# Causal attention with a routed feed-forward on one core: the softmax sums are accumulated on GpSimd and multiplied by ones once per step

## The chip, the core and the metric

One core of a Trainium2 chip runs the whole program. TensorE (PE) multiplies matrices into PSUM, VectorE (DVE) and ScalarE (ACT) do elementwise work, reductions and exponentials, GpSimd (POOL) does elementwise work on SBUF, and SyncE (SP) issues the transfers. Each engine works through its own queue of instructions; semaphores tie them together. The metric is the device time of one execution in microseconds (us), as the median of a few runs. One further execution is recorded by the profiler, and its instructions are what the views below show.

## The reference

The input x has two sequences of 2048 tokens with 512 features, all in float32. The layer is

- x = x + attention(layernorm(x)), with 16 heads of width 32, rotary positions on queries and keys, a causal mask and a softmax over the keys;
- x = x + ffn(layernorm(x)), where ffn is a 512x512 linear layer with a bias plus a routed low-rank part: eight experts of rank 16, of which a softmax router picks two per token.

The part that matters here is the softmax: for each query and head, the sum over all keys of exp(score - shift) times the value row, divided by the sum over all keys of exp(score - shift). The second sum, the denominator, is what the change moves.

## The kernel before, in words

The tokens are cut into eight **blocks** n = 0..7 of 512 (four per sequence; j = n mod 4 is the place of the block in its sequence), the heads into four **groups** g of four heads. A **step** (n, g) is the attention of one block's queries for one group, 32 steps in all. Step (n, g) looks at 4(j+1) **key tiles** of 128 keys: 4, 8, 12 or 16. The last four lie on the diagonal.

Work on one step has two passes. In the first (`row_maxima`, line 346) PE computes scores with queries on the partitions (`sm`, line 367) and DVE takes the row maxima (lines 375 and 380), which are turned (line 397) into a shift. In the second (`attend`, line 432) PE computes the scores again with keys on the partitions (`sc`, line 463), adds the shift by a small matmul (line 471), and ACT takes the exponential (line 485) into a buffer `pt` that holds one key tile for four heads, 128 x 4 x 512 in float32. On diagonal tiles POOL then sets the masked corner to zero, two heads at a time (line 494). PE multiplies the tile with the values into the PSUM bank `av` (line 519). The four heads of a group sit in different rows or columns of the PE array and run side by side; a float32 matmul shows as two records. The fourth diagonal tile shares a buffer with the second, so that a step of 16 tiles has 15 exponential stages, called quads.

The denominator: when both tiles of a pair (0,1), (2,3), ... have been multiplied, POOL adds the odd tile onto the even one in two instructions of two heads each (line 534), and three phases later PE multiplies the pair's sum by a 128x32 tile of ones into the PSUM bank `den` (`summed`, line 545), accumulating over the pairs. After the last pair ACT copies the sums out (line 554), a chain of small transfers with a reciprocal on DVE in between (lines 567 to 579) spreads 1/sum over the partitions, and POOL scales the context (line 581).

The order of PE, ACT and DVE is written out by the program: the second pass of a step runs beside the first pass of the next one, half a quad of each at a time (`side_by_side`, line 591), and after each half, called a phase, a loop (lines 733 to 763) may place other work. That is the value and denominator matmuls that have come due (`later`, `between`, `ahead`) and stages of other blocks, paced by a credit in us: projections of the next block (`kps`, `qps`, lines 182 to 201, whose rotary part ends with two POOL instructions; `vps`), and the output projection and feed-forward of the former block (`ops`, `xnps`, `mid`, `yps`, lines 227 to 340, with small POOL chains for the layernorm and the bias). These stages are called fillers below. The order of POOL and SP follows from it.

Buffers: `pt` has four (`PTS`). PSUM has a ring of six banks for scores and fillers (`bank`), beside `av` and `den`. `before()` (line 500) forces due work out of the list before the buffers that it holds are taken again. `wo` and `base_w`, the 1 MB weights of the output projection and of the linear layer, are loaded once at the start.

## Time and profile before

| | |
|---|---|
| median of 3 runs | 1982.68 us (1980.56 to 1984.05) |
| profiled execution, whole | 1982.82 us |
| its span | 1981.0 us |
| PE busy | 1918.0 us (97%) |
| PE weight loads | 731.2 us (37%) |
| POOL busy | 1008.7 us (51%) |
| DVE busy | 1018.2 us (51%) |
| ACT busy | 768.0 us (39%) |
| pair additions on POOL (line 534) | 320 instructions, 609.9 us busy |
| denominator matmuls (line 545) | 1280 records, 163.3 us busy |

Busy is the time in which at least one instruction of a kind ran. PE instructions overlap, so their mean times exceed what each adds: for 1280 records of the denominator the mean is 569 ns, but eight records that belong to one pair keep PE busy for about 1.1 us.

A step's end is easy to find in the timeline: the ACT copy of `av` at line 538. The stretches between these copies are called the steps' lengths below. For blocks 2 and 3, in us: (2,0) 61.3, (2,1) 77.8, (2,2) 65.6, (2,3) 75.5, (3,0) 82.8, (3,1) 92.7, (3,2) 79.7, (3,3) 75.7. For blocks 6 and 7: 61.3, 76.8, 65.6, 75.5, 81.7, 84.3, 72.8 and 54.4. They differ within a block because the fillers are not spread evenly. The last step has neither fillers nor a first pass beside it. What follows the last copy takes 52.2 us.

### The profile page before, as it was taken

How to read it: one execution, taken by the hardware profiler on the slowest of the kernel's cores; microseconds unless marked ns; L12 is line 12 of the kernel's file. 1: busy time of each engine (PE TensorE's matmuls, PEld its weight loads, DVE VectorE, ACT ScalarE, POOL GpSimd, SP SyncE). 2: the span in 40 equal slices, each digit the busy share in tenths (PEclk: the TensorE clock that was granted, in tenths of full speed). 3: DMA queues.
4: the chain of work that ended last, by engine and by line, in shares of the span. 5: the costliest groups of instructions: out<-in, count | busy, mean ns of one | idle time of the engine just before them, and what ended most of it. 6: DMA issues, size and time to landing. Idle time of an engine off the chain costs nothing.

```text
span 1981.0 us, 31399 instructions
## 1 busy us (share of the span) xinstructions
PE 1918.0 (97%) x12256; PEld 731.2 (37%) x12256; DVE 1018.2 (51%) x2760; ACT 768.0 (39%) x1601; POOL 1008.7 (51%) x906
## 2 busy tenths in 40 slices
PE   7999999999999999999999999999999999999997
PEld 3433433333333333333343434333433333333333
DVE  3555555555554655553255546446565555555403
ACT  1323342344433444353532334224434334443451
POOL 3545554455464555355565345435555545553572
PEclk9999999999999999999999999989999999999999
DMA  5000110000100000100000001100011000001000
GB/s 186 23 12 13 32 35 22 7 7 28 60 1 7 7 1 18 48 23 8 10 28 12 28 28 38 49 7 7 2 38 49 1 6 7 1 7 44 6 7 22
DMA packets 34861, 46.33 MB, mean 23 GB/s; under 512 B 12956, under 2 KB 13468, under 8 KB 34712
## 3 DMA queue, kind: packets, MB, share of 16 engines
q1 hardware_dynamic: 34712, 44.32, 7.0%
q8 instruction: 96, 1.57, 0.3%
q14 instruction: 53, 0.43, 0.1%
HBM read 35.40 MB, written 8.90 MB: 22 GB/s over the span
## 4 chain that ended last, share of the span: by engine, by line
PE 83%; POOL 7%; issue 4%; DVE 4%; ACT 1%; DMA 1%; SPq 0%; POOLq 0%; DVEq 0%
PE sm L367 24%; PE av L519 13%; PE den L545 6%; PE ops L239 6%; PE vps L210 6%; PE qps L185 5%; PE kps L185 5%; PE yps L320 5%; PE sc L471 5%; PE sc L463 4%; POOL pt L534 3%; POOL pt L494 2%; PE mid L265 1%; PE yps L327 1%; ACT pt L485 1%
## 5 line engine op out<-in xcount | busy, mean ns | idle before, releaser
L485 ACT ACTIVATE pt<-sc 128x512 f32<-128x512 f32 (+1 forms) x1152 | 595.1, 572 | 950.8 <-PE sc L471 882.0
L534 POOL TENSOR_TENSOR pt<-pt,pt 128x1024 f32<-128x1024 f32 (+2 forms) x320 | 609.9, 1920 | 339.2 <-ACT pt L485 193.6
L463 PE MATMUL sc<-q,k 32*128 32x512 f32 (+3 forms) x2560 | 677.5, 576 | 10.7 <-DVE parts L392 10.1
L367 PE MATMUL sm<-k,q 32*128 32x512 f32 (+3 forms) x2560 | 644.1, 574 | 6.3 <-POOL q L201 3.6
L380 DVE TENSOR_REDUCE pm<-sm 128x1 f32<-128x512 f32 x768 | 490.8, 685 | 286.5 <-PE sm L367 273.6
L367 PEld LDWEIGHTS sm<-k,q 32*128 32x128 f32 x2560 | 221.4, 184 | 375.0 <-issue 148.7
L519 PE MATMUL av<-pt,v 128*32 128x512 f32 (+3 forms) x2560 | 306.0, 550 | 19.1 <-POOL pt L494 14.2
L375 DVE CUSTOM_DVE_ANT_0 sm<-sm,mask 128x128 f32<-128x128 f32 (+3 forms) x512 | 245.8, 512 | 141.8 <-PE sm L367 118.7
L471 PE MATMUL sc<-max,ones_b 3*128 3x512 bf16 (+3 forms) x1280 | 261.2, 346 | 0.0
L463 PEld LDWEIGHTS sc<-q,k 32*128 32x128 f32 x2560 | 233.1, 185 | 51.2 <-issue 24.2
L494 POOL TENSOR_SCALAR_AFFINE_SELECT pt<-pt 128x256 f32<-128x256 f32 (+1 forms) x192 | 93.0, 485 | 154.7 <-ACT pt L485 152.2
L545 PE MATMUL den<-pt,ones 128*32 128x512 f32 (+1 forms) x1280 | 163.3, 569 | 0.0
L519 PEld LDWEIGHTS av<-pt,v 128*32 128x32 f32 x2560 | 57.5, 109 | 201.5 <-issue 142.1
L185 PE MATMUL kps<-xnt_a,wk 128*128 128x512 f32 x256 | 123.3, 626 | 5.0 <-ACT xnt_a L156 4.9
L239 PE MATMUL ops<-wo,ctx 128*128 128x512 f32 x256 | 120.2, 614 | 2.7 <-POOL ctx L581 2.7
L320 PE MATMUL yps<-base_w,xnt_f 128*128 128x512 f32 x256 | 116.9, 599 | 2.6 <-DVE pm L380 1.6
L185 PE MATMUL qps<-xnt_a,wq 128*128 128x512 f32 x256 | 118.3, 605 | 0.0
L210 PE MATMUL vps<-wv,xnt_a 128*128 128x512 f32 x256 | 117.5, 604 | 0.0
L471 PEld LDWEIGHTS <-ones_b 3*128 3x128 bf16 x1280 | 78.3, 94 | 101.0 <-issue 94.5
L200 POOL TENSOR_TENSOR sw_q<-sw_q,sin 128x512 f32<-128x512 f32 x32 | 40.7, 1273 | 112.5 <-DVE sw_q L198 112.5
L200 POOL TENSOR_TENSOR sw_k<-sw_k,sin 128x512 f32<-128x512 f32 x32 | 40.7, 1273 | 109.2 <-DVE sw_k L198 93.8
L581 POOL TENSOR_TENSOR ctx<-ctx,sum 128x512 f32<-128x512 f32 x32 | 40.6, 1268 | 90.1 <-DMA sum<-over 84.8
(85 smaller groups left out, 1246.4 us busy)
## 6 DMA issues: line engine op xcount, KB each, us to landing
xa<-in_x SPq DMA_DIRECT2D x32, 256.0 KB
xf<-in_x SPq DMA_DIRECT2D x32, 256.0 KB
out<-xf SPq DMA_DIRECT2D x32, 256.0 KB
sum<-over SPq DMA_DIRECT2D x124, 64.0 KB
cos<-in_cos SPq DMA_DIRECT2D x8, 256.0 KB
sin<-in_sin SPq DMA_DIRECT2D x8, 256.0 KB
sums<-sum SPq DMA_DIRECT2D x124, 2.0 KB
wk<-in_wk_t SPq DMA_DIRECT2D x1, 1024.0 KB
```

The source lines that it names most:

```text
L185: nc.tensor.matmul(out=pj, lhsT=w[:, c, bass.ts(g, P)], rhs=held["xn_t"][:, c, :], start=(c == 0), stop=(c == NC - 1),)
L210: nc.tensor.matmul(out=pv, lhsT=held["xn_t"][:, c, bass.ts(t, P)], rhs=wv[:, c, :], start=(c == 0), stop=(c == NC - 1),)
L239: nc.tensor.matmul(out=po, lhsT=ctx_t[c][:, bass.ts(t, P)], rhs=wo[:, c, :], start=(c == 0), stop=(c == NC - 1),)
L367: nc.tensor.matmul(out=sc[r][:, some[i]], lhsT=q[rows, bass.ts(ts[i], P)], rhs=keys[c][rows, : wide_of[i]], start=True, stop=True,)
L375: nc.vector.tensor_tensor_reduce(sc[r][:, here], sc[r][:, here], mask[:, BLK - w :], 1.0, 3.0 * MASKED, ALU.add, ALU.max, pm[:, t, r, c : ...
L380: nc.vector.reduce_max(pm[:, t, r, c : c + 1], sc[r], axis=AX.X)
L463: nc.tensor.matmul(out=sc[r][:, place(kts[i])], lhsT=keys[jj][rows, bass.ts(tt, P)], rhs=q[rows, low(kts[i]) :], start=True, stop=False,)
L471: nc.tensor.matmul(out=sc[r][:, place(kts[i])], lhsT=ones_b[rows, :], rhs=s["max"][rows, low(kts[i]) :], start=False, stop=True,)
L485: nc.scalar.activation(pt[:, r, all_of], sc[r][:, all_of], AF.Exp, scale=1.0 / math.sqrt(DK))
L519: nc.tensor.matmul(out=s["av"][rows, low(kt) :], lhsT=values[jj][g][:, tt, rows], rhs=pts[kt][:, r, place(kt)], start=(kt == 0), stop=(kt ...
L534: nc.gpsimd.tensor_add(some, some, pts[kt + 1][:, r : r + 2, place(kt + 1)])
L545: nc.tensor.matmul(out=s["den"][DK * r : DK * r + DK, lo:], lhsT=ones, rhs=pts[kt][:, r, lo:], start=(kt == 0), stop=(kt == tiles - 2),)
```

## The change: one running sum per step

Key tile 0 of a step now gets a buffer of its own kind, `acc` (two of them), and every other tile a `pt` buffer, of which there are three. As soon as the exponentials of two heads of a tile are there (and masked), POOL adds them onto `acc`; the first addition of a step waits until PE has multiplied tile 0 with the values, since that reads `acc` unchanged. After the last value matmuls of a step, one group of four matmuls by ones makes the denominator from `acc`, in a bank of the ring, which has seven banks now that `den` has none of its own. `wo` and `base_w` share one buffer and are loaded by turns, once per block each: `wo` with the first x tile of the block's finish, `base_w` after its last output projection.

```diff
-PTS = 4
+PTS = 3
-        return ps.tile(list(shape), dtype, tag=f"ps{banks[0] % 6}", name=name)
+        return ps.tile(list(shape), dtype, tag=f"ps{banks[0] % 7}", name=name)
...
-    wo = load_weight(wo_t, "wo")
-    base_w = load_weight(base_wt, "base_w")
+    def load_in_turn(src, name):
+        w = wide.tile([P, NC, D], F32, tag="w", name=name)
+        nc.sync.dma_start(out=w, in_=src.rearrange("(c p) o -> p c o", p=P))
+        return w
...
         def load(t):
             held["x"].append(load_x(n, t, True))
+            if t == 0:
+                held["w"] = load_in_turn(wo_t, f"wo_{n}")
...
-                    rhs=wo[:, c, :],
+                    rhs=held["w"][:, c, :],
...
+            if t == NT - 1:
+                held["w"] = load_in_turn(base_wt, f"base_w_{n}")
...
-                    rhs=base_w[:, c, :],
+                    rhs=held["w"][:, c, :],
...
+        pts, index, ready = {}, {}, []
+        s["first"] = False
...
                 if kts[0] not in pts:
+                    tag, bufs = ("pt", PTS) if kts[0] else ("acc", 2)
                     pt = p2.tile(
-                        [P, 4, BLK], F32, tag="pt", bufs=PTS, name=f"pt_{n}_{g}_{kts[0]}"
+                        [P, 4, BLK], F32, tag=tag, bufs=bufs, name=f"pt_{n}_{g}_{kts[0]}"
                     )
+                    begun[0] += kts[0] > 0
                     for kt in kts:
-                        index[kt], pts[kt] = begun[0], pt
-                    begun[0] += 1
+                        index[kt], pts[kt] = begun[0] if kts[0] else 1 << 30, pt
...
+                if kts[0] and r % 2:
+                    ready.extend((kt, r - 1) for kt in kts)
+                    add()
...
-                while any(tile <= begun[0] - PTS for _, tile, _, _ in due):
+                while kts[0] and any(tile <= begun[0] + 1 - PTS for _, tile, _, _ in due):
                     due.pop(0)[2]()
...
-                oldest = diagonal + 1 if kts[0] == tiles - 2 else kts[0] - kts[0] % 2
-                later(2, index[oldest], lambda: weighted(kts))
+                later(2, index[kts[0]], lambda: weighted(kts))
...
-            for kt in kts:
-                kt -= kt % 2
-                paired[kt] = paired.get(kt, 0) + 1
-                if paired[kt] == 2:
-                    lo = low(kt + 1)
-                    for r in (0, 2):
-                        some = pts[kt][:, r : r + 2, place(kt, lo)]
-                        nc.gpsimd.tensor_add(some, some, pts[kt + 1][:, r : r + 2, place(kt + 1)])
-                    later(3, index[kt], lambda kt=kt: summed(kt), 1)
+            if kts[0] == 0:
+                s["first"] = True
+                add()
             if kts[-1] == tiles - 2:
                 s["dest"] = wide.tile([P, BLK], F32, tag="ctx", bufs=6, name=f"ctx_{n}_{g}")
                 nc.scalar.copy(s["dest"], s["av"])
+                later(2, 1 << 30, summed)
 
-        def summed(kt):
-            lo = low(kt)
-            if kt == 0:
-                s["den"] = ps_o.tile([P, BLK], F32, tag="den", name=f"den_{n}_{g}")
+        def add():
+            while s["first"] and ready:
+                kt, r = ready.pop(0)
+                some = pts[0][:, r : r + 2, low(kt) :]
+                nc.gpsimd.tensor_add(some, some, pts[kt][:, r : r + 2, place(kt)])
+
+        def summed():
+            den = bank(f"den_{n}_{g}")
             for r in range(4):
                 nc.tensor.matmul(
-                    out=s["den"][DK * r : DK * r + DK, lo:],
-                    lhsT=ones,
-                    rhs=pts[kt][:, r, lo:],
-                    start=(kt == 0),
-                    stop=(kt == tiles - 2),
+                    out=den[DK * r : DK * r + DK, :], lhsT=ones, rhs=pts[0][:, r, :],
+                    start=True, stop=True,
                 )
-            if kt == tiles - 2:
+            if True:
                 total = p2.tile([P, BLK], F32, tag="tmp", bufs=5, name=f"sum_{n}_{g}")
-                nc.scalar.copy(total, s["den"])
+                nc.scalar.copy(total, den)
```

More of the change, by code (lines that the diff above doesn't have):

```diff
@@ L439, in attend @@
         together += [(diagonal + 1, diagonal + 3), (diagonal + 2,)]
-        pts, index, paired = {}, {}, {}
+        pts, index, ready = {}, {}, []
+        s["first"] = False
         def low(kt):
```

## The prediction

> **What bounds the kernel now.** I read the page's busy shares first, then the groups by line.

> ```profile
> PE 1918.0 (97%) x12256; PEld 731.2 (37%) x12256; DVE 1018.2 (51%) x2760; ACT 768.0 (39%) x1601; POOL 1008.7 (51%) x906
> ...
> L534 POOL TENSOR_TENSOR pt<-pt,pt 128x1024 f32<-128x1024 f32 (+2 forms) x320 | 609.9, 1920 | 339.2 <-ACT pt L485 193.6
> ...
> L545 PE MATMUL den<-pt,ones 128*32 128x512 f32 (+1 forms) x1280 | 163.3, 569 | 0.0
> ```

> PE has work nearly all the time, POOL half of it. The change takes most of 163 us from PE and adds to POOL, so the average says "faster". But POOL's work isn't spread evenly, so I read the additions by shape, and then both engines in five steps: (3,0), (3,1), (3,2), (7,2), (7,3).

> ```profile
> L534 POOL TENSOR_TENSOR pt<-pt,pt 128x1024 f32<-128x1024 f32 x192 | 448.9, 2354 | 279.9 <-ACT pt L485 193.6 <-PE av L519 86.0
> L534 POOL TENSOR_TENSOR pt<-pt,pt 128x768 f32<-128x768 f32 x64 | 116.0, 1812 | 6.8 <-PE av L519 1.5
> L534 POOL TENSOR_TENSOR pt<-pt,pt 128x256 f32<-128x256 f32 x64 | 45.0, 725 | 52.5 <-PE av L519 52.5
> ```

> ```profile
> core 0: us, PE busy (x) PEld busy (x) DVE busy (x) ACT busy (x) POOL busy (x), PEclk, DMA share, GB/s
> 659.80:742.60 82.80, 82.46 (x576) 28.95 (x575) 47.81 (x105) 36.52 (x70) 47.50 (x41) 1.00 0.02 4
> 742.60:835.30 92.70, 91.30 (x613) 32.68 (x608) 51.58 (x142) 37.07 (x79) 43.58 (x29) 1.00 0.09 30
> 835.30:915.00 79.70, 76.93 (x550) 26.66 (x542) 44.15 (x94) 38.91 (x75) 49.80 (x43) 1.00 0.07 21
> 1801.50:1874.30 72.80, 71.20 (x531) 23.26 (x524) 38.88 (x79) 34.27 (x67) 38.05 (x25) 1.00 0.07 23
> 1874.30:1928.80 54.50, 51.00 (x376) 17.36 (x380) 0.25 (x1) 29.23 (x60) 36.09 (x23) 0.95 0.02 6
> ```

> About 33 us of POOL's 36 to 50 are additions here. Last, the pace of each engine between fillers, in the timeline:

> ```profile
> 1849.83 1.07 PE L545 MATMUL den<-pt,ones 128*32 128x512 f32 x8
> 1850.83 0.69 PE L367 MATMUL sm<-k,q 32*128 32x512 f32 x1
> ...
> 1852.12 1.07 PE L519 MATMUL av<-pt,v 128*32 128x512 f32 x8
> 1853.11 0.69 PE L367 MATMUL sm<-k,q 32*128 32x512 f32 x1
> ```

> ```profile
> 1896.16 9.31 POOL L534 TENSOR_TENSOR pt<-pt,pt 128x1024 f32<-128x1024 f32 x4
> ```

> By starts, a pair's denominator takes PE 1.0 us, half a quad 1.25 and a value group 1.0; a bare quad is 3.5 (2.7 without a first pass beside it). Four additions take 9.31 us: 2.33 each, 4.67 for a full tile.

> [...]

> **The change part by part.**

> *PE.* 160 pair groups become 32: 128 x 1.0 = 128 us less (1.1 by busy time, 163.3/160 with the short ones).

> *POOL.* A step now adds every tile but the first: 576 instructions for 320. A full tile costs 4.67, the first diagonal one 4.67 + 2 maskings of 0.41 = 5.5, the shared buffer 2 x (0.64 + 1.80 + 0.71) = 6.3, the last 2 x (0.41 + 1.27) = 3.4. (No row has 128x512 additions of this line; 0.72 and 1.81 are the bounds, 1.27 us is line 201's of that size, which I take.) Additions in a step of 16 tiles rise from 33 to 64 us, of 12 from 24 to 45, of 8 from 14.5 to 26, of 4 from 5 to 7.7. Each kind of step occurs eight times: 8 x (64 + 45 + 26 + 7.7) = 1142 us for 610, and POOL's total becomes 1009 + 532 = 1541, 78% of the span, still below it.

> *Where POOL can't run ahead or behind.* Its order in the new program is, at a step's end: mask, add, mask, add, tile by tile. PE's last value group needs the last mask, so PE waits until POOL has done all the step's additions but one. Then no addition of the next step is there before PE has done tile 0's values: two or three half quads (1.25 each), the denominator (1.0) and that group (1.0), a *gap* of 5.8 us; 9.4 where a query projection (3.6) stands in it; 2.7 where no first pass runs. Within a step three `pt` buffers let PE be up to two tiles ahead, but not across this point. So a step in which POOL limits takes: gap + full tiles x 4.67 + other POOL work + 13.95 (diagonal, less the last 1.27) + 0.75 (last value group). Other work by its rows: rotary 2.6 (that of the projection in the gap is done within it), context 1.3, layernorm chain 1.24, bias 1.3 each.

> | step | gap + tiles + other + 14.7 | before |
> |---|---|---|
> | (3,0), (7,0) | 9.4 + 51.4 + 14.2 = 89.7 | 82.8, 81.7 |
> | (3,2) | 5.8 + 51.4 + 14.2 = 86.1 | 79.7 |
> | (3,3) | 2.7 + 51.4 + 6.6 = 75.4 | 75.7 |
> | (7,2) | 5.8 + 51.4 + 1.3 = 73.2 | 72.8 |
> | (7,3) | 2.7 + 51.4 + 1.3 = 70.1 | 54.5 |
> | (2,0), (6,0) | 9.4 + 32.7 + 11.6 = 68.4 | 61.3 twice |
> | (2,2), (6,2) | 5.8 + 32.7 + 14.2 = 67.4 | 65.6 twice |

> Together +55 us. PE's own sums there, with the fillers as the new order places them, are lower or level: (7,2) loses 9 us of fillers and 7 of denominators and would need 56; (3,0) gains 8 and would need 83.

> In the other long steps fillers come first and POOL's bare stretch last. (3,1), (7,1): gap 9.4, tile 2 with a transpose and a router matmul 4.9, tiles 3 to 5 with a feed-forward group each 3 x 8.2, tile 6 with one 7.9, half a quad 1.25: PE reaches tile 7 after 48 us. With 1.2 for the exponentials and then 5 x 4.67 + 14.7 = 38 on POOL it is 87.3 against 92.7 and 84.3. (2,1), (6,1): by the same count the shared diagonal buffer starts at 60.6 and POOL needs 6.3 + 3.4 - 1.27 + 0.75 more: 70 against 77.8 and 76.8. (2,3), (6,3): gap 9.4, four quads 14, five projections 18.2, half a quad and exponentials 2.4, then 3 x 4.67 + 14.7: 72.8 against 75.5. Together -22. Blocks of 8 tiles save 3 x 1.0 of PE a step and give about 2 back at the diagonal: -7 in eight steps. Blocks of 4: -2 in all.

> *Seven banks, three buffers, acc.* PE stood idle only 63 us in all; the seventh bank may save some of it, next to nothing while PE waits for POOL. -1 with the tail, which has one denominator group less.

> *Weights by turns.* 16 loads of 1 MB. Between blocks the last `ops` and the first `yps` lie 40 us apart: hidden. [...] On SP the `base_w` load waits for the last `ops` ahead of a sums chain that is issued later: nothing late.

> *Sum.* 55 - 22 - 9 - 1 = +23 on the profiled execution's 1982.8 (span 1981.0 and 1.8 around it), which is the median too: 2005.

> **The rivals.**
> - *PE's saving rules*: POOL's backlog is absorbed and the gaps fill with its other work, so each step takes the larger of PE's and POOL's sums: (3,0) 84, (3,2) 81, (7,2) 68, (7,3) 68, and so on, in all -74: 1908. For it: POOL's 78%. Against: the mask order and the wait for tile 0, both in the program. It decides if the gap and the tail of the diagonal cost below 3 us a step instead of 6 to 10; halved they give about 1955. Chance 0.21 for below 1978.7.
> - *The queues behind POOL*: layernorm chains and rotary parts now lie behind additions, ACT waits for `mom`, DVE for a free `tmp` buffer, PE for them; 2 us in each of 16 long steps more: 2035 and up. For it: DVE's stream shuffle already waits 20 us for line 534. Against: two tiles of lead. Chance 0.15.
> - *A draw*: gaps a third shorter than I count leave 1982. Chance 0.06 within 0.2% (4 us, about what a measurement tells from no change).

> My forecast, POOL as the limit of the long steps (1987 to 2030), has 0.58. So faster 0.21, same 0.06, slower 0.73. The range leaves a tenth on each side: 1955, the halved gaps, to 2032; the likeliest case's own is 1990 to 2025.

> **What would show it.** POOL busy near 1540 us, its additions near 1140; 256 records of the denominator, some 35 us; PE idle rising by over 100 us, ended by POOL in lines of values (masks) and exponentials waiting for additions; the last step near 70 us; step (2,1) shorter. I am wrong if the last step stays near 55, if long steps fall below 80 in blocks 3 and 7, if an addition into `acc` doesn't take 2.33 us, or if a weight load ends a wait of PE.

## The result and the profile after

The changed kernel takes 2040.46 us (median of four runs, 2036.19 to 2043.76) and the kernel before, timed beside it, 1981.85: a ratio of 1.0293, with a 95% interval of 1.027 to 1.0317. It is slower by 59 us, where 23 were forecast. The direction and the tie between the engines were right; the size was not, and 2040 lies outside the range given.

The page of the kernel before has this chain of work that ended last (shares of the span), and this group for the value matmuls (busy us, mean ns of one | idle just before, and what ended it):

```profile
PE 83%; POOL 7%; issue 4%; DVE 4%; ACT 1%; DMA 1%; SPq 0%; POOLq 0%; DVEq 0%
...
L519 PE MATMUL av<-pt,v 128*32 128x512 f32 (+3 forms) x2560 | 306.0, 550 | 19.1 <-POOL pt L494 14.2
```

The page of the changed kernel, with its busy line, its chain, and below them three groups by line:

```profile
PE 1881.8 (92%) x11232; PEld 729.7 (36%) x11232; DVE 1012.4 (50%) x2760; ACT 766.9 (38%) x1601; POOL 1531.3 (75%) x1162
...
PE 66%; POOL 22%; issue 8%; DVE 2%; ACT 2%; DMA 0%; SPq 0%; POOLq 0%; DVEq 0%; ACTq 0%
```

```profile
L551 POOL TENSOR_TENSOR pt<-pt,pt 128x1024 f32<-128x1024 f32 (+2 forms) x576 | 1137.5, 1993 | 173.2 <-ACT pt L496 145.3 <-PE av L531 8.3
L531 PE MATMUL av<-pt,v 128*32 128x512 f32 (+3 forms) x2560 | 331.3, 593 | 104.4 <-POOL pt L505 104.0 <-ACT ctx L543 0.2
...
L556 PE MATMUL den<-pt,ones 128*32 128x512 f32 x256 | 36.3, 619 | 0.0
```

POOL's 1531 us, the additions' 1137, and 256 records of the denominator with 36 us are what the prediction gave (1540, 1140, 35). PE lost 127 us of denominators, and yet its busy time fell by only 36. Most of the other 91 came back as slower matmuls: PE was at work for 208 us at half clock, for 50 before, and a value group that takes 1.07 us at full clock takes 1.94 there; as an estimate, that makes 70 to 80 us. PE now also stands idle 104 us in front of values (19 before), and what it waits for there is line 505, the masks on POOL. The chain shows the shift: POOL's share was 7% before and is 22% now.

Of the additions, the 128x512 form, for which the prediction had to take 1.27 us from another line, takes 1.268.

```profile
L551 POOL TENSOR_TENSOR pt<-pt,pt 128x512 f32<-128x512 f32 x64 | 81.1, 1268 | 5.2
```

The windows of the same five steps as before, (3,0), (3,1), (3,2), (7,2), (7,3), and last of (1,0), which has 8 tiles (start:end, length, busy time of each engine, granted clock):

```profile
core 0: us, PE busy (x) PEld busy (x) DVE busy (x) ACT busy (x) POOL busy (x), PEclk, DMA share, GB/s
675.00:766.00 91.00, 85.62 (x552) 32.71 (x548) 50.33 (x123) 38.80 (x77) 81.35 (x58) 0.96 0.05 16
766.00:854.90 88.90, 86.37 (x524) 31.87 (x520) 47.98 (x124) 34.30 (x71) 69.76 (x39) 0.92 0.16 48
854.90:942.80 87.90, 76.87 (x502) 27.66 (x498) 43.59 (x94) 38.97 (x74) 78.82 (x55) 0.92 0.04 13
1845.90:1920.90 75.00, 65.53 (x462) 23.33 (x466) 36.41 (x76) 34.23 (x66) 67.06 (x37) 0.90 0.02 5
1920.90:1990.00 69.10, 55.71 (x316) 14.64 (x308) 0.25 (x1) 29.02 (x59) 66.72 (x37) 0.73 0.02 5
171.10:220.80 49.70, 44.37 (x261) 16.39 (x262) 23.12 (x63) 15.91 (x31) 36.30 (x28) 0.83 0.03 7
```

POOL is now busy 67 us of the last step's 69 and 79 of 88 in (3,2). The clock column (PEclk, 1.00 is full speed) shows what the prediction had not: before, it stood at 1.00 in four of the five steps. TensorE's clock records have 52 us at half speed in the kernel before and 254 us in the changed one.

The end of step (7,1) and the start of (7,2) on POOL, from the timeline (start, length):

```profile
1841.80 0.41 POOL L505 TENSOR_SCALAR_AFFINE_SELECT pt<-pt 128x256 f32<-128x256 f32 x1
1842.29 1.26 POOL L551 TENSOR_TENSOR pt<-pt,pt 128x512 f32<-128x512 f32 x1
1843.51 0.41 POOL L505 TENSOR_SCALAR_AFFINE_SELECT pt<-pt 128x256 f32<-128x256 f32 x1
1844.00 1.27 POOL L551 TENSOR_TENSOR pt<-pt,pt 128x512 f32<-128x512 f32 x1
1852.97 4.67 POOL L551 TENSOR_TENSOR pt<-pt,pt 128x1024 f32<-128x1024 f32 x2 [7.70 <-ACT pt L496]
```

The order mask, addition, mask, addition is as described, a full tile is 4.67, and the gap stands in the last line: POOL stands idle for 7.70 us. On PE the same stretch reads:

```profile
1844.78 1.08 PE L531 MATMUL av<-pt,v 128*32 128x256 f32 x8
...
1849.43 1.06 PE L556 MATMUL den<-pt,ones 128*32 128x512 f32 x8
...
1851.72 1.07 PE L531 MATMUL av<-pt,v 128*32 128x512 f32 x8
```

The step ends with the value group at 1844.78; the denominator stands 4.65 us later and the group of tile 0, without which the program lets no addition begin, 2.3 us after that. That group ends at 1852.79, 0.2 us ahead of the addition. The line above names an exponential, which ended 0.1 us later still; so it is from the program that the group's place is known to count, and the trace alone can't tell the two apart.

### The profile page after: what moved, and what is told of

Same layout as the page of the kernel before. It is cut to its first block, busy times and chain, and to the rows that moved or that the text cites. A ratio compares the mean times of both kernels' runs of the same rounds, so it can differ in the third digit from the quotient of the medians.

```text
span 2040.5 us, 29922 instructions
## 1 busy us (share of the span) xinstructions
PE 1881.8 (92%) x11232; PEld 729.7 (36%) x11232; DVE 1012.4 (50%) x2760; ACT 766.9 (38%) x1601; POOL 1531.3 (75%) x1162
## 4 chain that ended last, share of the span: by engine, by line
PE 66%; POOL 22%; issue 8%; DVE 2%; ACT 2%; DMA 0%; SPq 0%; POOLq 0%; DVEq 0%; ACTq 0%
PE sm L375 19%; POOL pt L551 15%; PE av L531 9%; PE qps L189 6%; PE yps L328 5%; PE vps L214 5%; PE kps L189 5%; PE ops L245 4%; PE sc L473 4%; PE sc L481 3%; POOL pt L505 2%; PE den L556 2%; PE yps L335 1%; ACT pt L496 1%; POOL k L205 1%
## 5 line engine op out<-in xcount | busy, mean ns | idle before, releaser
L551 POOL TENSOR_TENSOR pt<-pt,pt 128x1024 f32<-128x1024 f32 (+2 forms) x576 | 1137.5, 1993 | 173.2 <-ACT pt L496 145.3
L473 PE MATMUL sc<-q,k 32*128 32x512 f32 (+3 forms) x2560 | 727.6, 606 | 16.9 <-DVE pm L383 8.0
L531 PE MATMUL av<-pt,v 128*32 128x512 f32 (+3 forms) x2560 | 331.3, 593 | 104.4 <-POOL pt L505 104.0
L473 PEld LDWEIGHTS sc<-q,k 32*128 32x128 f32 x2560 | 248.2, 197 | 109.5 <-issue 34.5
L481 PE MATMUL sc<-max,ones_b 3*128 3x512 bf16 (+3 forms) x1280 | 274.2, 359 | 0.0
L189 PEld LDWEIGHTS qps<-xnt_a,wq 128*128 128x128 f32 x256 | 47.4, 195 | 71.9 <-issue 57.5
L189 PEld LDWEIGHTS kps<-xnt_a,wk 128*128 128x128 f32 x256 | 47.7, 196 | 70.5 <-issue 60.4
```

The costliest lines, as they stand in the source:

```text
L189: nc.tensor.matmul(out=pj, lhsT=w[:, c, bass.ts(g, P)], rhs=held["xn_t"][:, c, :], start=(c == 0), stop=(c == NC - 1),)
L473: nc.tensor.matmul(out=sc[r][:, place(kts[i])], lhsT=keys[jj][rows, bass.ts(tt, P)], rhs=q[rows, low(kts[i]) :], start=True, stop=False,)
L481: nc.tensor.matmul(out=sc[r][:, place(kts[i])], lhsT=ones_b[rows, :], rhs=s["max"][rows, low(kts[i]) :], start=False, stop=True,)
L531: nc.tensor.matmul(out=s["av"][rows, low(kt) :], lhsT=values[jj][g][:, tt, rows], rhs=pts[kt][:, r, place(kt)], start=(kt == 0), stop=(kt ...
L551: nc.gpsimd.tensor_add(some, some, pts[kt][:, r : r + 2, place(kt)])
```

## The experiments

### Which part costs the time

*e1, before with one part of the change: weights loaded by turns.*

```
-    wo = load_weight(wo_t, "wo")
...
+            if t == 0:
+                held["w"] = load_in_turn(wo_t, f"wo_{n}")
...
+            if t == NT - 1:
+                held["w"] = load_in_turn(base_wt, f"base_w_{n}")
```

> The kernel before with one part of the change alone: wo and base_w share a buffer and are loaded by turns, 16 loads of 1 MB. Theory A (POOL's order and rate make the change slow): the loads are hidden, so 1982 us within 4. Rival C (the loads collide with the sums' transfers or hold up SP, and that is part of the loss): 1990 us or more, with waits of PE that a weight load ends.

Measured: 1983.69 us, ratio 0.9999 (0.9986 to 1.0012). The loads are hidden. In the trace of the kernel after, the packets of the last one (issued at 2009.1) end 5.7 us after its issue.

*e2, after without the additions of heads 2 and 3* (their denominators are left incomplete).

```
             while s["first"] and ready:
                 kt, r = ready.pop(0)
+                if r:
+                    continue
```

> The changed kernel without the additions for heads 2 and 3 of each group (their denominators then hold key tile 0 alone): 288 additions instead of 576, all else in place. Theory A: a full tile costs POOL 2.33 us instead of 4.67, less than PE's 3.5, so PE limits again and the saved denominators show: 1870 to 1910 us, POOL busy near 960, the last step near 45 us instead of 69. Rival C (three pt buffers, the ring or the weights cost the time): 1990 or more, with little change from 2040.

Measured: 1861.77 us, ratio 0.9398 (0.9381 to 0.9416); POOL busy 974 us, PE 97%, half clock 26 us. With half of the additions gone the kernel takes 179 us less, three times the whole loss, while buffers, banks and PE's order stay as they are: the loss comes from the additions.

*e6, after without the masks on POOL, the denominator two phases later* (the masked corners are left as they are).

```
-                if kts[0] >= diagonal and r % 2:
...
-                    nc.gpsimd.affine_select(
...
-                later(2, 1 << 30, summed)
+                later(4, 1 << 30, summed)
```

> The changed kernel without the 192 masking instructions, so that the diagonal tiles keep their forbidden corner, and with the denominator two phases later. All 576 additions stay. PE's last value groups then wait for no POOL instruction. Theory A (it is the masks queued behind additions that tie PE to POOL at a step's end, and the gap that follows): POOL runs through the gaps, long steps come down to POOL's own sum less the masks, (3,0) near 80, (7,3) near 65, and the whole to 1920 to 1970 us. Rival B (POOL's rate alone): 93 us of masks less on POOL and nothing else, 2000 or more.

Measured: 1907.96 us, ratio 0.9629 (0.961 to 0.9648). The page's busy line and the value matmuls:

```profile
PE 1831.0 (96%) x11232; PEld 725.0 (38%) x11232; DVE 1008.9 (53%) x2760; ACT 764.6 (40%) x1601; POOL 1438.6 (76%) x970
...
L520 PE MATMUL av<-pt,v 128*32 128x512 f32 (+3 forms) x2560 | 304.3, 556 | 1.3 <-ACT ctx L532 1.2
```

POOL still does all the additions and is busy 1439 us, as large a share of the span as in the kernel after, but the values wait for it no more (1.3 us for 104): 132 us less in all. The later denominator alone is worth 26 of these (e14, below). The other 107 have two possible causes that this run changes together: PE's wait for the masks, and the 94 us of masks that POOL needn't do. Two things speak for the wait as a cause of its own. In the eight steps of 8 tiles, where POOL is busy only two thirds of the time, e6 takes 34.8 us less than e14 while POOL does 22.5 us less. And in e9, below, the masks leave POOL too but still end after its additions, and nothing is gained. How the 107 us divide is not shown.

*e8, after with only the full tiles added; the diagonal's tiles and the sum are multiplied by ones right after the last value group.*

```
-                if kts[0] and r % 2:
+                if 0 < kts[0] < diagonal and r % 2:
...
-                later(2, 1 << 30, summed)
+                summed()
...
+            rest = sorted({0, *range(diagonal, tiles)})
+            for kt in rest:
```

> The changed kernel with the additions of the four diagonal tiles taken out: only tiles 1 to d-1 are added onto the sum of tile 0, and PE multiplies the sum and the four diagonal tiles by ones straight after the last value group (3.8 us a step for 1.0). POOL has 384 additions, all of full tiles and all ahead of the masks, about 1285 us in all. Theory A: the tie at a step's end is nearly gone and PE does 3 instead of 8 pair groups in a step of 16: 1870 to 1930 us, clock above 0.97, faster than the kernel before. Rival B (three buffers and the rate of 4.67 us per full tile limit the long steps anyway): 1970 or more.

Measured: 1990.41 us, ratio 1.0057 (1.0034 to 1.008). A miss: POOL's load fell to 1178 us and PE's waits for its masks from 104 to 33, but 1216 of the 1280 old denominator records are back, many of them short (101 us busy for 163 before), so PE has less left to save. It is the nearest of the complete variants to the kernel before, and not faster.

### POOL's order

In the kernel after the planner places POOL's instructions. *e3* fixes POOL's order as the program is written, as a control for the next two:

```
-    manual_schedule(engines={et.PE, et.Activation, et.DVE})
+    manual_schedule(engines={et.PE, et.Activation, et.DVE, et.Pool})
```

> The changed kernel with POOL's order written out as the program emits it, instead of being left to the planner; the same instructions. It is the control for the next run. Theory A: the masks still stand behind the additions at a step's end, so 2040 us within 10. If the planner's order was itself the fault: below 2010.

Measured: 2057.55 us, ratio 1.0391 (1.0371 to 1.041), 17 us over the kernel after.

*e4, on e3: all masks ahead of the diagonal's additions, the denominator at four phases (with a second buffer for `few`).*

```
-                    add()
+                    masked[0] += kts[0] == tiles - 2
+                    if kts[0] < diagonal or masked[0] == 2:
+                        add()
...
-                later(2, 1 << 30, summed)
+                later(LATE, 1 << 31, summed)
```

> The changed kernel with POOL's order written out, all masks of a step ahead of the additions of its diagonal tiles, and the denominator two phases later. The same additions, so POOL is as busy (about 1530 us), but PE's last value groups no longer wait for additions, and these fill the gap at the start of the next step. Theory A (the coupling at a step's end costs 6 to 10 us a step): 1910 to 1950 us, step (3,0) near 84 and (7,3) near 68. Rival B (POOL's rate within a step alone is what costs, wherever the gap is): 2020 or more. With theory D (the lower granted clock of PE, 0.938, comes from these waits) the clock is back above 0.97.

Measured: 2118.32 us, ratio 1.0682 (1.065 to 1.0714), 61 us over its control: the forecast fell. The waits (us in total, times, longest):

```profile
POOL pt L507 <- ACT pt L498: 210.4, 87, 8.6
...
PE den L562 <- POOL pt L557: 69.2, 9, 11.2
PE av L537 <- POOL pt L507: 62.4, 25, 10.1
```

PE's wait for masks fell from 110 us in e3 to 62, but POOL, which has nothing to do between two masks now, waits 210 us for exponentials (57 in e3), and does the held additions afterwards, where the denominator waits 69 us for them. The idle moved from PE into POOL's queue, and POOL has none to spare.

*e7, on e3: the diagonal's additions held back by one tile only, the denominator at three phases.*

```
+                    if kts[0] < diagonal:
                         ready.extend((kt, r - 1) for kt in kts)
+                    else:
+                        ready.extend(held.pop(0) if len(held) > 1 else [])
+                        held.append([(kt, r - 1) for kt in kts])
...
-                later(2, 1 << 30, summed)
+                later(3, 1 << 30, summed)
```

> As the run with POOL's order written out (2058 us), with the additions of each diagonal tile held back by one tile, so that a mask stands behind one tile's additions less, and the denominator one phase later. Theory A: the stall of PE at the last masks shrinks by 2 to 4 us a step and the last additions fill the gap: 1970 to 2020 us. If, as in the run with all masks first, POOL then waits for exponentials at the diagonal what it saves in the gap: 2040 or more.

Measured: 2023.48 us, ratio 1.0203 (1.0175 to 1.0231), 34 us below its control and 3 above the range of theory A. The run changes two things, and a later denominator gains by itself in the planner's order (e14, below), so it isn't shown how much of the 34 us the held additions bring.

### Other engines for the masks

*e9 and e10, after with the masks as multiplications on VectorE, the denominator at four and at two phases.*

```
+                    for kt in kts:
+                        on = pt[:, r - 1 : r + 1, place(kt)][:, :, :P]
+                        nc.vector.tensor_mul(on, on, kept[:, None, :].to_broadcast([P, 2, P]))
...
```

> The kernel after with the masks on VectorE: each half buffer's corner is multiplied in place by a triangle of ones and zeros, one operation for each tile and head pair (256 of 128x256), and the denominator comes four phases after the last value group, as in the kernel without masks. Nothing of the computation is left out. Theory A (the masks queued behind POOL's additions are the tie): PE's last value groups no longer wait for the additions, the time is near the 1908 of the kernel without masks, 1910 to 1950, and waits of value groups on POOL vanish. Rival B (VectorE's own queue is tied to POOL by rotary operations and normalizations that wait for POOL's results, so the masks only change queues): 1975 to 2040, value groups waiting for VectorE's multiplications.

> The same with the denominator two phases after the last value group, as in the kernel after. If the place of the denominator matters as long as POOL is behind (A): 5 to 25 us slower than with four phases, PE waiting ahead of the denominator for POOL's additions. If POOL has caught up by then (B): within 4 us.

Measured: 2019.27 us, ratio 1.0192 (1.0177 to 1.0207), and 2036.12, 1.0273 (1.0258 to 1.0288). Rival B won in the first, A in the second (17 us). Against the kernel with the denominator at the same place, the masks on VectorE change little: 2019 for the 2015 of e14, 2036 for 2040. Two pieces of e9's timeline, POOL and VectorE, show how the masks meet POOL again:

```profile
434.54 2.34 POOL L550 TENSOR_TENSOR pt<-pt,pt 128x1024 f32<-128x1024 f32 x1
```

```profile
434.67 2.50 DVE L508 TENSOR_TENSOR pt<-pt,kept 128x256 f32<-128x256 f32 x1
```

POOL's addition ends at 434.54 + 2.34 = 436.88; the multiplication, begun at 434.67, at 437.17. Of the 256 multiplications, the 100 that began while POOL did no two-operand work took 0.42 us each; 140 took more than 0.45, 1.21 on average, and 138 of these ended 0.27 to 0.29 us after the POOL operation that ran when they began. In these a mask on VectorE still ends after the addition that it was meant to get away from, and VectorE's row maxima stand behind it in its queue (PE's scores wait 23 us for them, 8 in the kernel after). Why it ends so late is not shown. That PE's direct waits for VectorE's masks are only 17 us says that these late endings are not all of the 111 us between e9 and e6; the rest isn't resolved.

*e11, the kernel before with the same masks.*

> The kernel before with the same masks on VectorE: how much of a gain is the masks' alone. There POOL keeps up, and PE waits for its masks by 32 and 14 us in all. Theory A: 1965 to 1983. If the masks cost the kernel before as much as the one after, it gains over 40 us: below 1942.

Measured: 1999.64 us, ratio 1.0093 (1.0077 to 1.011), a loss of 19 us. Moving the masks costs time where POOL keeps up.

*e17, the masks on VectorE with one buffer operand: added to the scores in their bank, ahead of the exponentials.*

```
+                for kt in kts if kts[0] >= diagonal else ():
+                    corner = sc[r][:, place(kt)][:, :P]
+                    nc.vector.tensor_add(corner, corner, below)
...
-                later(2, 1 << 30, summed)
+                later(4, 1 << 30, summed)
```

> The masks on VectorE ahead of the exponentials: the corner of each head's scores gets the mask added in its bank (512 additions of 128x128, of one buffer operand each, 0.3 us by the like operation of the first pass), [...]; the denominator four phases late. Nothing of the computation is left out. [...] If VectorE's queue as such (1198 us busy there, about 1170 here) is what holds the exponentials and values: 1985 or more.

Measured: 2041.0 us, ratio 1.0303 (1.0258 to 1.0347); 1925 to 1970 was expected if the late endings of e9's multiplications were what kept it at 2019. The additions took 0.305 us, and at most 0.335 beside POOL's additions, so that none ended late as e9's multiplications did, and the waits moved once more:

```profile
ACT pt L505 <- PE sc L487: 498.3, 326, 6.8
ACT pt L505 <- DVE sc L504: 479.6, 176, 7.4
```

The exponentials wait for the masks in VectorE's order, behind its row maxima; the 1985 or more of VectorE's queue holds. (The denominator is at four phases here and in e15, so the 2015 us of e14 are what to hold these two against.)

*e15, the masks on PE, added to the scores ahead of the shift.*

```
+                    if kts[i] >= diagonal:
+                        nc.tensor.matmul(out=sc[r][:, place(kts[i])][:, :P],
+                            lhsT=mask[:, BLK - P :], rhs=ident_b, start=False, stop=False)
...
-                later(2, 1 << 30, summed)
+                later(4, 1 << 30, summed)
```

> The kernel after with the masks on TensorE: 512 bfloat16 multiplications of 128x128 add the first pass's mask to the scores' diagonal corners ahead of the exponentials, and nothing of POOL's or VectorE's order stands between exponentials and values; the denominator comes four phases after the last value group. Nothing of the computation is left out. Theory A (the masks behind the additions, on POOL, [...] are the tie): the 1908 of the kernel without masks and 512 x 0.06 to 0.12 us, 1935 to 1970, below the kernel before. Rival (POOL at 76% with the additions is a limit by itself, whoever masks): 1985 or more.

Measured: 2274.27 us, ratio 1.1472 (1.1447 to 1.1498), the worst miss.

```profile
PE 2231.6 (98%) x11744; PEld 850.4 (37%) x11744; DVE 1025.4 (45%) x2760; ACT 765.8 (34%) x1601; POOL 1441.1 (63%) x970
```

POOL isn't the limit here: PE is busy 400 us longer than without masks, 0.78 us for each of 512 multiplications that show 0.25 (those of the same size that turn the row maxima, `mps`, kept PE busy 0.10 us each in the kernel before). A good part of it is half clock (428 us for 85). Scores and the first pass's products run four at a time, each in its own 32 rows of the array (four records start within 0.03 us in the kernel after). In e15's trace the masks of all 128 rows split these fours: between two masks stand two pairs of records, 0.43 us apart, so that a stretch that served four serves two. By form, the scores of 384, 256 and 128 columns kept PE busy 134, 123 and 64 us for 75, 74 and 32 in the kernel after, while the mean of one record rose only from 596 to 608, 527 to 572 and 282 to 335 ns. That this is the rest of the 400 us is the reading of such stretches; no run isolates it.

### PE's own terms: the bank, the clock, the denominator

*e12, after with six banks in the ring.*

```
-        return ps.tile(list(shape), dtype, tag=f"ps{banks[0] % 7}", name=name)
+        return ps.tile(list(shape), dtype, tag=f"ps{banks[0] % 6}", name=name)
```

> The kernel after with six banks in the ring. PE waits for POOL there, not for banks, so theory A: within 6 us of the kernel after, 2034 to 2046. If the seventh bank hides part of the loss, over 2050; if it lets the first pass and the projections run ahead into POOL's gaps and so does harm, below 2034.

Measured: 2101.66 us, ratio 1.0598 (1.0537 to 1.0658): 61 us more. The seventh bank, which the prediction counted at next to nothing, hides as much again as the change costs. Half-clock time rose to 360 us. The pieces of the chain that ended last which are PE's and lie in half-clock records come to about 46 us before, 152 after and 267 in e12. Half of the 115 us between the last two is 57, close to the 61 lost: by this arithmetic, which no run tests, the lost bank is paid for in PE at half speed.

*e5, after with PE kept busy by six bfloat16 multiplications ahead of the last two value groups of each step.*

```
+            if kts[0] > diagonal:
+                spin = bank(f"spin_{n}_{g}_{kts[0]}")
+                for _ in range(6):
+                    nc.tensor.matmul(out=spin, lhsT=ones_b, rhs=mask, start=True, stop=True)
```

> The changed kernel with six bf16 matmuls of 128x128 by 128x512 into an unread bank of the ring (about 1.3 us together by the line 481 rows, 0.2 each) ahead of the value matmuls of the second and third diagonal quad of every step, where PE now waits for masks. Theory D (PE's clock is halved for 253 us because PE stands idle there, and that is the part of the loss which the steps' sums miss): granted clock above 0.965 and 2005 to 2030 us. Rival (the clock's fall costs nothing, since POOL limits there anyway): 2040 to 2110 us, up to 64 x 1.3 = 83 more.

Measured: 2064.63 us, ratio 1.0418 (1.04 to 1.0436); half clock fell to 163 us. This decides nothing: the multiplications stood where PE mostly didn't wait (24 of the 64 places had a wait of 0.9 us or more), and took a bank of the ring, which e12 shows to be dear.

*e13, the same idea placed by the trace: multiplications by zeros into the values' own bank, in the 39 places where PE waited 0.9 us or more, as many as fill the wait.*

```
...
+            for _ in range(SPINS.get((n, g, kts[0] - diagonal), 0) if kts[0] else 0):
+                nc.tensor.matmul(out=s["av"], lhsT=zeros_b, rhs=mask, start=False, stop=False)
```

> The kernel after, with TensorE kept busy in its own waits: ahead of each value group that waited 0.9 us or more there (39 of them) stand as many bfloat16 multiplications by zeros as fill the wait, 353 in all, added into the bank of the values (they add zero, and take no bank of the ring). Theory C (the lower granted clock after such waits is a good part of the loss: the chain that ended last holds 152 us of TensorE at half clock, for 46 before): half-clock time falls from 254 us to under 160, and the kernel gains 15 to 45 us: 1995 to 2025. Rival (the half clock lies where POOL sets the pace anyway): the half-clock time falls as much, and the time stays within 6 us of 2040 or rises by the multiplications that overshoot, to 2060.

Measured: 2027.45 us, ratio 1.0223 (1.0207 to 1.0238), 13 us below the kernel after with 353 matmuls more. The granted clock is 0.972 in the mean for 0.938, with 116 us at half clock for 254. PE's wait for masks in front of the values fell from 104 to 50 us, as the multiplications by zeros took its place. The clock is a part of the loss, a little less than theory C's lower end. In the trace of the kernel after, the 40 half-clock records last multiples of 3.4 us, but for the last, which lies after the span, and before each of the other 39 PE stood idle for 0.7 us or more in all within 3.4 us. Short waits are among these: 1.3 us in front of a value group of step (6,1), with 0.4 us a little earlier, was followed by 6.8 us at half clock. Not every wait was: of the 54 idle stretches of 0.9 us or more, 38 had half clock within 3.4 us after their end.

*e14, after with the denominator at four phases.*

```
-                later(2, 1 << 30, summed)
+                later(4, 1 << 30, summed)
```

> The kernel after with one edit: the denominator comes four phases after the last value group instead of two. With the masks on VectorE that was worth 17 us. If the denominator, standing in TensorE's order ahead of work that could run, waits for POOL's last additions (a wait that the prediction left out): 2015 to 2030. If the masks hold TensorE back first, so that the additions are done by then: 2036 to 2045.

Measured: 2014.79 us, ratio 1.0174 (1.0148 to 1.0201), 26 us less. Not for the reason expected: PE hardly waits at the denominator for POOL, in either kernel. It is the gap that shrinks. The denominator took its own place in the order of due work, and the value group of tile 0 came a half quad after it (the 2.3 us between 1849.43 and 1851.72 above). Placed later, it lets that group go first: the first addition after steps (3,1), (6,1) and (7,1) comes 3.9, 4.0 and 3.9 us after the step's end, for 6.2, 7.3 and 7.0.

*e16, e13's and e14's edits together* (248 multiplications, placed by e14's waits).

> The kernel after with both edits that gained by themselves: the denominator four phases after the last value group (2014.8 alone), and TensorE kept busy in its waits of that order by 248 multiplications by zeros (the like gained 13 us alone). If both are separate terms of what the prediction missed (35 us), they add up: 1997 to 2006, the predicted 2005. If they are one and the same loss, seen twice: 2011 to 2020.

Measured: 2003.16 us, ratio 1.0116 (1.0095 to 1.0137): 37 us less than the kernel after, where the single edits gave 13 and 26. So they are largely separate terms. No version that does the whole computation came out below the kernel before.

## Why the prediction was wrong

By its own terms, with the lengths of the steps summed by their number of tiles (change against the profiled execution of the kernel before, in us):

| steps of | forecast | after | e13 | e16 |
|---|---|---|---|---|
| 16 tiles | +34.6 | +41.3 | +43.4 | +36.1 |
| 12 tiles | -2.2 | +7.6 | +2.2 | -8.8 |
| 8 tiles | -7 | +17.7 | +5.3 | +3.0 |
| 4 tiles, tail | -3 | -7.0 | -5.4 | -15.9 |
| sum | +23 | +59.6 | +45.5 | +14.4 |

- *PE's saving* was right: 127 us of denominators went.
- *POOL's additions* were right in number, duration and sum, the unseen 128x512 form too.
- *The coupling at a step's end* is there: the trace has the order mask, addition, mask, addition, and 104 us of PE's waits for those masks, and e6 has neither the waits nor the loss. How much of e6's gain is the coupling and how much POOL's lighter load is not divided.
- *The table of POOL-limited steps* held within 3 us, with +64 for +55: (3,0) 91.0 and (7,0) 90.0 for 89.7, (3,2) 87.9 for 86.1, (3,3) 74.9 for 75.4, (7,2) 75.0 for 73.2, (7,3) 69.1 for 70.1, (2,0) and (6,0) 68.3 and 70.3 for 68.4, (2,2) and (6,2) 68.2 and 70.2 for 67.4. Its gaps were a little short: 5.8 for a measured 6.2 to 7.3; with a projection in it 9.4 for 9.2 to 10.3.
- *The step that failed* is "Blocks of 8 tiles save 3 x 1.0 of PE a step and give about 2 back at the diagonal: -7". It measured +17.7 and makes 25 of the missing 37 us. The saving was nearly right: the denominators of these eight steps took 20 us less (24 forecast). What came back was not 2 us a step but nearly 5. PE's idle time in the eight steps rose from 9 to 29 us, nearly all of it waits for masks (3.5 to 23.9), and its work at half clock from 17 to 52 us, which costs about 16 more, as an estimate from the 1.94 us of a value group for 1.07. Waits, slower matmuls and saving make +16, of 17.7 measured. So two terms were put too low: the wait for POOL at the diagonal, since its limit was worked out from 12 tiles up only, and the clock, since all pieces of the sum were at full speed. For (1,0) the same formula gives 9.4 + 3 x 4.67 + 3.9 + 14.7 = 42.0, already over the 38.6 of before; the step took 49.8, with a gap of 12.9, a clock of 0.83 and one output tile more in it than before. (The fillers only changed places: over the eight steps their numbers are the same within 1%, but for five small matmuls.) The runs agree: filling the waits (e13) took 12.4 us out of these eight steps, and without masks and with the later denominator (e6) they take 21 us less than before, and PE has hardly a wait there (7 us idle).
- *The long steps* make another 16 us, 9 in the table and 7 in the mixed steps (-15 for -22), about 1 us a step. e13 took back 5 in the steps of 12 tiles and nothing in those of 16: there POOL sets the pace whatever PE's clock, and the short gaps are the likelier cause. e14, which shortens the gaps, takes 13 us out of the steps of 12 tiles and 7 out of those of 16, but no run isolates the forecast's error in the gaps. Short steps and tail gave 4 more back than forecast.
- *"The seventh bank ... next to nothing"* was a wrong reason: e12 puts it at 61 us. The sum didn't show it, since the bank is part of the change; without it the kernel would have been at 2102.
- *The weights* were right (e1).
- *The rival "queues behind POOL"* gave 2035 and up, and the time is there, but its mechanism is only a small part of what was found. ScalarE waits 24 us for the layernorm chain on POOL (1 before), and PE 10 us more for ScalarE there; exponentials wait 45 us for additions (9 before), and PE 5 us for those. The masks hold PE for 90 us more than before. What the rivals lacked is that PE, having waited, was often slower afterwards: 208 us of its work lay at half clock, for 50 before.
- *"PE's saving rules"* named 1908, and e6 takes 1908. That is luck: e6 leaves 94 us of masks out and has a later denominator, and the rival's sum had neither.

That e16 lands on 2003, by the predicted 2005, is not a proof of the sum: its later denominator is a better order than the one that was predicted, and e13 alone leaves 22 us over the forecast.

## What to carry to other kernels

Before work is moved to another engine, ask which of that engine's instructions others wait for soon (here 94 us of masks), and what will stand ahead of them. Its busy share doesn't answer that: POOL was at 75% of the span in the kernel after and at 76% in e6, which is 132 us faster. Work out the limit of the loaded engine for every size of step, the short ones too, and count waits that you put on TensorE twice: once as waits, and once as slower matmuls after them (here 104 us idle in front of values for 19, and 208 us of work at half clock for 50). With POOL's queue overfull, reordering it or handing the masks to a third engine mostly moved the wait or cost more elsewhere (e4 came out 61 us over its control; e9, e15 and e17 4, 259 and 26 over e14); less work on it (e2, 179 us less), or an earlier start of its work (e14, 26 less), shortened the time.
